# Sparse attention over 2708 rows on one core: the fullest tiles' last slots as a tile of their own, light tiles first, more turning on VectorE, s3 and C22 on GpSimd

## The chip, the cores and the metric

The kernel runs on one core of a Trainium2 chip. The metric is the device time of one execution in microseconds. A core has TensorE (PE, with its weight loads as PEld), VectorE (DVE), ScalarE (ACT), GpSimd (POOL) and SyncE (SP, which here only issues DMAs).

## The reference

```python
h = jnp.maximum(_layernorm(x, axis=-1), 0.0)      # x: 2708 x 1024
q = h @ W_q.T + b_q
k = h @ W_k.T + b_k
v = h @ W_v.T + b_v
z = scale * (q @ k.T)
spare_z = z * adj                                 # adj: 2708 x 2708 of 0 and 1, density 0.0014771
spare_z = jnp.where(spare_z == 0.0, -10000.0, spare_z)
attn = jax.nn.softmax(spare_z, axis=1)
out = x + jax.nn.relu(attn @ v)
```

A row has some four neighbours on average. So the scores are only worked out at the edges, and the sum over neighbours is taken over rows of h; the product with W_v comes after it.

## The kernel before, in words

The rows are sorted by their number of neighbours in two groups (tiles 0 to 7, and 8 to 21), 128 rows to a tile. `K[t]` is the number of neighbour slots of tile t: 15, 7, 6, 5, 4, 4, 3, 2 for the first group and 15, 7, 6, 6, 5, 5, 4, 4, 4, 3, 3, 2, 1, 0 for the second. Tiles 0 and 8 are the fullest.

**TensorE.** After a stage on the weights (until about 100 us), the work goes in 20 units of two row tiles each, then one tile alone. Ten q units multiply h by M = W_q'W_k (with what belongs to it); ten o units multiply u, the weighted sums of neighbour rows, by W_v. A unit is a 2 x 2 block product with seven instead of eight products (`multiply`, L1027 to L1050): operands a11, a12, a22 and the sums s1 to s4, weights M and T (T is `wlow` in the trace), banks X, Y, Z (`ps`, `psy`). Each product is an `add_block`, which the trace shows as 8 matmul records of L987. The results are C11, C12 (`c12`, L1071 for q and L1102 for o: Z plus u2), C22 (`c22`, L1068 and L1098: Y plus p5) and C21. In the o units, ACT copies Y first (`taken`), and VectorE adds p5.

**Turning.** The operands are needed transposed. A tile that is not *faced* is turned by PE (`pt<-ident,u`, eight matmuls, L405), ACT copies a11, a12 and a22 from PSUM (L705), and VectorE forms s1 and s3 from the transposed block in PSUM (L709). A tile in `FACED` is copied in another order by ACT (v, L921), stored in `u_dram`, read back by four DMAs of 128 KB (`by_quarters`, L682 to L687, tile `or`), and turned by VectorE in 32 x 32 squares (`STREAM_TRANSPOSE`, L692). Ten tiles are faced: 6, 5, 4, 3, 2, 0, 1, 20, 18, 19. In `lower` (L725 to L737) s1 = a22 + a21, s3 = a11 − a21, s2 = s1 − a11, s4 = a12 − s2. If a tile of the unit is faced, s2 and s4 run on GpSimd, and s3 on VectorE (L729); else all four run on VectorE.

**The attention stream.** For each tile: `fetch` asks for its q rows (pq) and neighbour rows, `fill` (L839) has GpSimd gather one slot of 128 rows of h at a time (L600, 512 KB) into 13 row buffers (g0 to g10 and two in M's place), `scores` (L854) makes one VectorE operation per slot (`junk`, L860, with an accumulator), ACT takes the exponent, `weights` (L880) normalises, `sums` (L909) adds one slot per VectorE operation (u, L913). A tile of more than 8 slots scores its first slots, gives their buffers back, and gathers those rows again for the sum. The generator `attention` does this in the order of the list `order` (6, 5, 4, 3, 2, 0, 1, 7, 13, 12, 11, 10, 14, 9, 15, 16, 20, 17, 18, 19, 8); it also sets the o units' pairs, and tile 8 is the one alone. `advance(share)` (L1210 to L1213 for the share) lets the stream go on by some 20 / 7 or 19 / 7 us in each of the seven steps of a unit, less 0.75 / 7 for each faced tile of the next unit. VectorE executes in that order, by hand.

**Around it.** GpSimd also adds x to each result by a gather with addition (`add_x`, L1086, y) and scatters it (L812, out_dram), all in program order. Stores of q rows (L1061), reads of pq (L833), the read-back of u (L687) and the loads of the W_v weights into M and T (L1292: M00, T0, T1, M10, M11, T2, T3 in steps of the last q unit) go through SyncE in program order.

Of the kernel before, what the change touches and what calls it, by code (L numbers as in the profile page):

```python
# [10 lines left out]
FT = mybir.dt.float32  # L11
# [26 lines left out]
FACED = (6, 5, 4, 3, 2, 0, 1, 20, 18, 19)  # L38
# [28 lines left out]
def tile_preln_masked_attention(  # L67
# [25 lines left out]
    K = slot_counts(EARLY * P, EARLY) + slot_counts(N - EARLY * P, FULL - EARLY)[:-1] + [1, 0]  # L93
    PW = N // PARTS
# [12 lines left out]
    u_dram = dram.tile([FULL * P, D], FT, name="u_dram")  # L107
    m_dram = dram.tile([2, 2, P, 4, NB], FT, name="m_dram")
# [515 lines left out]
    def reload(lo, hi):  # L624
# [4 lines left out]
        if hi > FULL:  # L629
            loads.append(nc.gpsimd.dma_start(ptab[:REST, FULL, :], src[(FULL - lo) * P:, :]))  # L630
# [67 lines left out]
    def blocks(xa, xb, eng=None):  # L698
# [25 lines left out]
        def lower():  # L724
            if is_faced(xb):  # L725
# [3 lines left out]
                behind.append(nc.vector.tensor_sub(ops["s3"], ops["a11"], ops["s3"]))  # L729
# [94 lines left out]
    def fetch(t):  # L824
# [54 lines left out]
    def weights(t):  # L879
# [7 lines left out]
        if t in EMPTY:  # L887
# [12 lines left out]
        else:  # L900
            with tc.issue_after(chain[-1].ins):
                nc.vector.scalar_tensor_tensor(w[:, :k], w[:, :k], 1.0, ok, op0=ALU.mult, op1=ALU.mult, accum_out=m[:, 1:2])
                nc.vector.reciprocal(m[:, 3:4], m[:, 1:2])
                chain.append(nc.vector.tensor_scalar(coef[:, :k], w[:, :k], m[:, 3:4], None, op0=ALU.mult))  # L904
            nc.scalar.activation(u, g_of[t][0], AF.Copy, scale=coef[:, at[t][0]:at[t][0] + 1])  # L905
            free.append(g_of[t][0])
        us[t] = u, coef

    def sums(t):  # L909
        u, coef = us.pop(t)  # L910
        for s in range(0 if t in EMPTY else 1, K[t]):
            fill()
            chained(lambda: nc.vector.scalar_tensor_tensor(  # L913
                u, g_of[t][s], coef[:, at[t][s]:at[t][s] + 1], u, op0=ALU.mult, op1=ALU.add))
# [611 lines left out]
```

## Time and profile before

| what | value |
|---|---|
| median of 3 runs | 644.42 us (643.57 to 645.74) |
| the profiled execution's own time | 642.46 us |
| its span | 640.7 us |
| mean granted TensorE clock | 0.996 |
| bytes moved by DMA | 189.00 MB |
| gathers of h into g and M | 105 and 20 |
| DMAs issued by SyncE to read u back, of 128 KB | 40 |

A line of the timeline has the start and the length in us, the engine, the line of kernel.py, the operation, out<-in, the shape, and in brackets the idle time of the engine ahead of it with what ended it. A group's line has the count, then busy us and the mean ns of one, then idle time with its releasers.

### The profile page before, as it was taken

The numbers are of one execution on the slowest core, as the hardware profiler recorded it, in microseconds if no ns is written. First come the engines' busy times: TensorE is split into PE (matmuls) and PEld (weight loads), VectorE is DVE, ScalarE is ACT, GpSimd is POOL, SyncE is SP. The second block draws the span as 40 slices with busy tenths as digits, with TensorE's granted clock in tenths as the row PEclk, the third lists the DMA queues.
The fourth block names the chain that finished last, engine by engine and source line by source line (L and its number), as shares of the span: only waits on it lengthen the run. The fifth ranks groups of instructions, "written<-read, shape, count | busy, mean of one in ns | idle before, by whom it ended". The sixth has DMA issues, their size and how long they took to land.

```text
span 640.7 us, 6299 instructions
## 1 busy us (share of the span) xinstructions
PE 630.0 (98%) x1651; PEld 318.6 (50%) x1651; DVE 535.9 (84%) x1022; ACT 282.2 (44%) x420; POOL 398.4 (62%) x412
## 2 busy tenths in 40 slices
PE   9999999999999999999999989999999999999996
PEld 5777766444445444444444434444444434444442
DVE  5999889897895765989888998899999989999621
ACT  3448984859675532434232123333342426422300
POOL 2649960975768457745744836578674877873533
PEclk9999999999999999999999989999999999999999
DMA  8999996598798969997996999998997999986354
GB/s 337 406 352 319 352 361 265 203 342 317 248 367 311 369 194 401 371 370 249 274 310 243 326 419 288 343 277 251 341 313 251 270 346 289 283 266 193 72 164 145
DMA packets 66305, 189.00 MB, mean 295 GB/s; under 512 B 11181, under 2 KB 16637, under 8 KB 65368
## 3 DMA queue, kind: packets, MB, share of 16 engines
q0 software_dynamic: 27888, 84.95, 41.8%
q1 hardware_dynamic: 32874, 84.12, 37.5%
q10 hardware_dynamic: 5502, 19.48, 7.7%
q8 instruction: 15, 0.25, 0.2%
q14 instruction: 26, 0.21, 0.1%
HBM read 159.81 MB, written 42.31 MB: 315 GB/s over the span
## 4 chain that ended last, share of the span: by engine, by line
PE 18%; DVE 16%; issue 12%; DMA 9%; POOL 4%; ACT 0%; POOLq 0%; DVEq 0%
PE ps L987 10%; PE psy L987 7%; DVE junk L860 6%; DVE u L913 6%; DMA g<-h_dram,tab 3%; DMA pq<-q_late 3%; POOL g L600 2%; DMA or<-u_dram 2%; DMA qr<-h_dram,tab 2%; DVE s L709 1%; POOL M L600 1%; DMA pq<-q_dram,tab 1%; PE pt L405 1%; POOL qr L602 0%; DVE a L692 0%
## 5 line engine op out<-in xcount | busy, mean ns | idle before, releaser
L600 POOL DMA_INDIRECT g<-h_dram,tab x105 | 128.0, 1219 | 53.4 <-issue 19.2
L987 PE MATMUL ps<-M,a 128*128 128x512 f32 x320 | 145.8, 599 | 2.8 <-DMA M<-in_wv_dram 2.8
L987 PE MATMUL psy<-wlow,s 128*128 128x512 f32 x320 | 143.9, 592 | 0.0
L860 DVE SCALAR_TENSOR_TENSOR junk<-g,pq 128x1024 uint8<-128x1024 f32 x93 | 115.9, 1246 | 3.5 <-DMA g<-h_dram,tab 1.0
L913 DVE SCALAR_TENSOR_TENSOR u<-g,coef,u 128x1024 f32<-128x1024 f32 x79 | 106.1, 1343 | 5.2 <-ACT u L905 3.1
L987 PEld LDWEIGHTS ps<-M,a 128*128 128x128 f32 x320 | 60.1, 192 | 73.9 <-issue 69.9
L987 PEld LDWEIGHTS psy<-wlow,s 128*128 128x128 f32 x320 | 59.6, 190 | 69.7 <-issue 68.9
L379 DVE FIND_INDEX8 at<-ones,adj 128x8 uint32<-128x685 f32 (+1 forms) x88 | 74.5, 864 | 0.0
L987 PE MATMUL ps<-wlow,s 128*128 128x512 f32 x160 | 72.0, 593 | 1.2 <-DVE s L709 1.2
L987 PE MATMUL psy<-wlow,a 128*128 128x512 f32 x160 | 72.0, 593 | 0.0
L987 PE MATMUL ps<-M,s 128*128 128x512 f32 x160 | 71.9, 592 | 0.0
L358 ACT ACTIVATE sized<-adj 128x2708 uint8<-128x2708 f32 (+1 forms) x22 | 54.2, 2466 | 6.7 <-DMA adj<-in_adj_dram 5.4
L288 POOL TENSOR_TENSOR hsum<-hsum,x 128x256 f32<-128x256 f32 (+1 forms) x56 | 38.6, 724 | 26.6 <-DVE wlow L434 22.1
L987 PEld LDWEIGHTS ps<-wlow,s 128*128 128x128 f32 x160 | 30.3, 190 | 39.7 <-issue 39.3
L987 PEld LDWEIGHTS psy<-wlow,a 128*128 128x128 f32 x160 | 30.3, 190 | 38.5 <-issue 36.8
L987 PEld LDWEIGHTS ps<-M,s 128*128 128x128 f32 x160 | 30.3, 190 | 38.3 <-issue 37.5
L1086 POOL DMA_INDIRECT y<-in_x_dram,tab x19 | 31.0, 1633 | 14.7 <-issue 4.4
L812 POOL DMA_INDIRECT out_dram<-y,tab x21 | 27.9, 1330 | 15.4 <-DMA y<-in_x_dram,tab 9.9
L600 POOL DMA_INDIRECT M<-h_dram,tab x20 | 22.9, 1145 | 12.8 <-ACT u L905 4.7
L616 POOL DMA_INDIRECT tab_dram<-tab,pos_i x22 | 22.4, 1018 | 11.7 <-DVE pos_i L676 6.2
L266 ACT ACTIVATE x<-x,r 128x1024 f32<-128x1024 f32 (+1 forms) x22 | 25.8, 1232 | 6.1 <-POOL r L256 6.1
L905 ACT ACTIVATE u<-g,coef 128x1024 f32<-128x1024 f32 x16 | 18.4, 1148 | 21.9 <-DVE coef L904 20.8
(240 smaller groups left out, 871.4 us busy)
## 6 DMA issues: line engine op xcount, KB each, us to landing
adj<-in_adj_dram SPq DMA_DIRECT2D x21, 1354.0 KB, 12.2
x<-in_x_dram SPq DMA_DIRECT2D x21, 512.0 KB, 11.0
h_dram<-x ACTq DMA_DIRECT2D x21, 512.0 KB, 7.4
q_late<-q SPq DMA_DIRECT2D x12, 512.0 KB, 4.6
pq<-q_late SPq DMA_DIRECT2D x12, 512.0 KB, 4.9
u_dram<-v ACTq DMA_DIRECT2D x10, 512.0 KB, 5.6
or<-u_dram SPq DMA_DIRECT2D x40, 128.0 KB, 12.2
g<-in_wv_dram SPq DMA_DIRECT2D x16, 256.0 KB, 8.3
```

What stands on the lines that cost most here:

```text
L266: nc.scalar.activation(xs[i][:n], xs[i][:n], AF.Relu, bias=r[:n, 4, i:i + 1], scale=r[:n, 3, i:i + 1])
L288: small.append(nc.gpsimd.tensor_add(hsum[:n, cols], hsum[:n, cols], xt[:n, cols]))
L358: nc.scalar.activation(sized[:n], a[:n, :, :PW], AF.Abs, accum_out=total[:n, t:t + 1])
L379: nc.vector.max_index(at[:n, k - first_k, g, :], ones[:n, 0:8], a[:n, g, :])
L600: return nc.gpsimd.indirect_dma_start(out=dst, out_offset=None, in_=src, in_offset=off, bounds_check=N - 1, oob_is_err=False)
L616: put = nc.gpsimd.indirect_dma_start(out=tab_dram[lo >= EARLY][:, :], out_offset=bass.IndirectOffsetOnAxis(ap=pos_i[:n, t:t + 1], axis=0), ...
L812: to = nc.gpsimd.indirect_dma_start(out=out, out_offset=bass.IndirectOffsetOnAxis(ap=ptab.bitcast(U32)[:n, t, SLOTS:SLOTS + 1], axis=0), i ...
L860: chained(lambda: nc.vector.scalar_tensor_tensor(junk, g_of[t][s], 1.0, tq[t], op0=ALU.mult, op1=ALU.mult, accum_out=zall[:, t, s:s + 1]))
L905: nc.scalar.activation(u, g_of[t][0], AF.Copy, scale=coef[:, at[t][0]:at[t][0] + 1])
L913: chained(lambda: nc.vector.scalar_tensor_tensor(u, g_of[t][s], coef[:, at[t][s]:at[t][s] + 1], u, op0=ALU.mult, op1=ALU.add))
L987: mm = nc.tensor.matmul(bank, a[:, c, :], b[:, c, :], start=False, stop=(c == 3), skip_group_check=True)
L1086: return nc.gpsimd.indirect_dma_start(out=y[:n], out_offset=None, in_=x, in_offset=off, compute_op=ALU.add)
```

## The change

Four things are done together.

- *A second tile.* `K[0]` and `K[8]` become 8. Slots 8 to 14 of the first 64 rows of tiles 0 and 8 form tile 21 (`SECOND`, 7 slots; upper half of the partitions from tile 8, `HP` = 64). It is treated by the attention stream just ahead of tile 0: its weighted sum is not normalised and goes to `v_dram`, its sum of weights (`mass`) is moved from partitions 64 to 127 to partitions 0 to 63 by a small DMA. Tiles 0 and 8 add the mass to theirs, and a last operation of 64 rows adds the rows read from `v_dram`. No tile gathers rows twice any more (14 gathers fewer, and 7 more for tile 21).
- *The order* becomes 6, 5, 4, 3, 2, 1, 0, 7, 20, 19, 18 and so on down to 9, and 8 alone.
- *Faced tiles* are found as the stream goes: every tile finished before step 2 of the unit two ahead of its own. This makes 18; tiles 11, 9 and 8 are not faced.
- *GpSimd* takes s3 of faced units (L743 now) and C22 of the o units (L1140 now). The share of an o unit's steps is 19 / 7 always. The q rows of tiles 18 and 19 are stored through ACT's queue.

The diff, cut to its core:

```diff
-FACED = (6, 5, 4, 3, 2, 0, 1, 20, 18, 19)
...
+    HOSTS = (0, EARLY)
+    SECOND = NT - 1
+    HP = P // 2
+    VK = K[0] - WIDE
+    for t in HOSTS:
+        K[t] = WIDE
...
+        loads.append((nc.gpsimd if lo >= EARLY else nc.sync).dma_start(
+            ptab[part, SECOND, 0:SLOTS + 1 - WIDE], src[0:HP, WIDE:SLOTS + 1]))
...
-                behind.append(nc.vector.tensor_sub(ops["s3"], ops["a11"], ops["s3"]))
+                nc.gpsimd.tensor_sub(ops["s3"], ops["a11"], ops["s3"])
...
+        if t == SECOND:
+            gather(tq[t][:HP], q_dram[:, :], t, SLOTS - WIDE, HP)
+            nc.sync.dma_start(tq[t][HP:], q_late[:HP, :])
...
+            if s == K[t]:
+                half = slice(HOSTS.index(t) * HP, (HOSTS.index(t) + 1) * HP)
+                nc.gpsimd.dma_start(g[:HP], v_dram[half, :])
...
-            if s < k - WIDE:
-                free.append(g_of[t][s])
...
-        if k > WIDE:
-            g_of[t] = g_of[t][k - WIDE:]
-            wanted.extend((t, s) for s in range(k - WIDE))
...
+        if t == SECOND:
+            coef = w
+            with tc.issue_after(chain[-1].ins):
+                chain.append(nc.vector.scalar_tensor_tensor(w[:, :k], w[:, :k], 1.0, ok, op0=ALU.mult, op1=ALU.mult,
+                                                            accum_out=mass[:, 0:1]))
+            nc.sync.dma_start(mass[:HP, 1:2], mass[HP:, 0:1])
...
+                if t in HOSTS:
+                    second = HOSTS.index(t)
+                    nc.vector.tensor_add(m[:HP, 1:2], m[:HP, 1:2], mass[:HP, second:second + 1])
...
+        if t in HOSTS:
+            chained(lambda: nc.vector.scalar_tensor_tensor(
+                u[:HP], g_of[t][K[t]][:HP], m[:HP, 3:4], u[:HP], op0=ALU.mult, op1=ALU.add))
...
+        if t == SECOND:
+            nc.sync.dma_start(v_dram, u)
+            return
+        unit = next((n for n, pair in enumerate(units) if pair[0] == "o" and t in pair[1:]), len(units))
+        if now < [unit - 2, 2] and t != alone:
+            faced_tiles.add(t)
+        if t in faced_tiles:
...
-    order = [6, 5, 4, 3, 2, 0, 1, 7, 13, 12, 11, 10, 14, 9, 15, 16, 20, 17, 18, 19, 8]
+    order = [6, 5, 4, 3, 2, 1, 0, 7, 20, 19, 18, 17, 16, 15, 14, 13, 12, 11, 10, 9, 8]
...
-    stream = attention(order)
+    stream = attention(order[:order.index(0)] + [SECOND] + order[order.index(0):])
...
-            (nc.scalar if t < 4 else nc.sync).dma_start(dst, q)
+            (nc.scalar if t < 4 or t >= BARE - 2 else nc.sync).dma_start(dst, q)
...
-            nc.vector.tensor_add(p5, copied(Y), p5)
+            nc.gpsimd.tensor_add(p5, copied(Y), p5)
...
-            share -= 0.75 / 7 * len(set(nxt[1:]) & set(FACED))
+            share = 19.0 / 7
```

Three places show how the order of instructions changes. The first is GpSimd's between the results of the first two o units (units 10 and 11), where the operands of unit 12 are formed. Here y is an add_x, out_0_dram a scatter, g and M gathers of neighbour rows. Before:

```order
L1086 DMA y_5_2445<-in_x_dram,tab_97 128x1024
L812 DMA out_0_dram<-y_6_2444,tab_97 2708x1024
L709 TENSOR_TENSOR s2_2622<-s1_2619,a11_2585 128x512
L709 TENSOR_TENSOR s4_2624<-a12_2587,s2_2622 128x512
L600 DMA g7_1406<-h_dram_63,tab_97 128x1024
L1086 DMA y_4_2577<-in_x_dram,tab_97 128x1024
L812 DMA out_0_dram<-y_5_2445,tab_97 2708x1024
L600 DMA M_145<-h_dram_63,tab_97 128x1024 x2
L600 DMA g8_1407<-h_dram_63,tab_97 128x1024
```

After the change:

```order
L611 DMA g1_1405<-h_dram_63,tab_98 128x1024
L611 DMA g3_1407<-h_dram_63,tab_98 128x1024
L743 TENSOR_TENSOR s3_2645<-a11_2593,s3_2645 128x512
L723 TENSOR_TENSOR s2_2650<-s1_2647,a11_2593 128x512
L723 TENSOR_TENSOR s4_2652<-a12_2595,s2_2650 128x512
L1140 TENSOR_TENSOR p5_2552<-taken_2710,p5_2552 128x512
L611 DMA g4_1408<-h_dram_63,tab_98 128x1024
L1128 DMA y_4_2563<-in_x_dram,tab_98 128x1024
L826 DMA out_0_dram<-y_5_2444,tab_98 2708x1024
L611 DMA g5_1409<-h_dram_63,tab_98 128x1024
L611 DMA g6_1410<-h_dram_63,tab_98 128x1024
L611 DMA g7_1411<-h_dram_63,tab_98 128x1024
```

s3 now stands ahead of s2 and s4, and the C22 of unit 11 (p5 with taken) behind them; the gathers g4 to g7 follow it in the queue, where before g7 and two gathers into M came right after s4.

The second place is VectorE's in a later o unit: the lower operands of unit 16 (before tiles 14 and 9, now 16 and 15) are formed while unit 15's C12 is due. Here pt is a transposed block in PSUM, `or` a tile read back, junk2 a score, u_ a sum, u2 of ps1 the C12. Before:

```order
L913 TENSOR_SCALAR u_16_3237<-M_145,coef_3236,u_16_3237 128x1024 x2
L913 TENSOR_SCALAR u_16_3237<-g8_1407,coef_3236,u_16_3237 128x1024
L709 TENSOR_TENSOR s1_3275<-a22_3268,pt_3270 128x512
L709 TENSOR_TENSOR s3_3277<-a11_3226,pt_3270 128x512
L709 TENSOR_TENSOR s2_3279<-s1_3275,a11_3226 128x512
L709 TENSOR_TENSOR s4_3281<-a12_3233,s2_3279 128x512
L860 TENSOR_SCALAR junk2_3288,zall_102<-g10_1409,pq_17_3242 128x1024
L860 TENSOR_SCALAR junk2_3290,zall_102<-g0_1399,pq_17_3242 128x1024
L1102 TENSOR_TENSOR u2_3259<-ps1_3135,u2_3259 128x512
```

After the change:

```order
L941 TENSOR_SCALAR u_12_3209<-g4_1408,coef_3208,u_12_3209 128x1024
L941 TENSOR_SCALAR u_12_3209<-g5_1409,coef_3208,u_12_3209 128x1024
L941 TENSOR_SCALAR u_12_3209<-g6_1410,coef_3208,u_12_3209 128x1024
L706 STREAM_TRANSPOSE a22_3256<-or_15_3167 128x4x4x32
L706 STREAM_TRANSPOSE s3_3258<-or_15_3167 128x4x4x32
L723 TENSOR_TENSOR s1_3260<-a22_3256,s3_3258 128x512
L941 TENSOR_SCALAR u_12_3209<-g7_1411,coef_3208,u_12_3209 128x1024
L881 TENSOR_SCALAR junk2_3279,zall_103<-g0_1404,pq_10_3228 128x1024
L1144 TENSOR_TENSOR u2_3246<-ps1_3143,u2_3246 128x512
```

Two transposes from `or_15` and one addition stand where four additions and subtractions stood; s3, s2 and s4 are no longer in VectorE's list.

The third place is SyncE's around the loads of the W_v weights (`wlow` is T, M from `in_wv_dram` the halves M10 and M11). Before:

```order
L687 DMA or_3_2379<-u_dram_66 32x4x256 x4
L1292 DMA wlow_168<-tv_dram_68 128x2048
L1061 DMA q_late_65<-q_18_2325 128x1024
L1292 DMA M_145<-in_wv_dram 128x2048 x2
L1292 DMA wlow_168<-tv_dram_68 128x2048
L1061 DMA q_late_65<-q_19_2326 128x1024
L1292 DMA wlow_168<-tv_dram_68 128x2048
```

After the change:

```order
L1103 DMA q_late_65<-q_17_2152 128x1024
L1335 DMA wlow_172<-tv_dram_69 128x2048
L1335 DMA M_149<-in_wv_dram 128x2048
L906 DMA mass_115<-mass_115 64x1
L701 DMA or_4_2378<-u_dram_66 32x4x256 x4
L701 DMA or_3_2383<-u_dram_66 32x4x256 x4
L954 DMA v_dram_67<-u_21_2355 128x1024
L1335 DMA M_149<-in_wv_dram 128x2048
L1335 DMA wlow_172<-tv_dram_69 128x2048 x2
```

T1 and M10 now follow the store of q_17 directly, without the store of q_18 ahead of M10; M11, T2 and T3 follow the move of mass, the read-back of tiles 4 and 3, and the store of u_21.

More of the change, by code (lines that the diff above doesn't have):

```diff
@@ L159, in tile_preln_masked_attention @@
     msq = const.tile([P, 9 + NT], FT, name="msq")
+    mass = const.tile([P, 2], FT, name="mass")
     nc.vector.tensor_copy(past, rows_i)
@@ L1203, in tile_preln_masked_attention @@
         kind, ta, tb = unit
-        now[0] = n
+        now[:] = n, 0
         if n == FIRST:
```

48 lines of the change are left out of this document (32 added, 16 removed).

## The prediction

> **What bounds the kernel now.** First the busy times of the page, then the windows of the o units (345 to 597 us) and of the tail.
>
> ```profile
> PE 630.0 (98%) x1651; PEld 318.6 (50%) x1651; DVE 535.9 (84%) x1022; ACT 282.2 (44%) x420; POOL 398.4 (62%) x412
> 345.00:597.00 252.00, 247.80 (x633) 113.39 (x632) 239.24 (x357) 83.52 (x143) 171.01 (x126) 0.99 0.93 294
> 597.00:640.70 43.70, 38.42 (x97) 17.11 (x95) 11.74 (x28) 6.55 (x12) 16.15 (x14) 0.98 0.50 140
> ```
>
> The columns of a window are its length and the busy time of PE, PEld, DVE, ACT and POOL, then the granted clock, the DMA share and GB/s. PE is busy 98% of the span, so the kernel looks bound by TensorE. But between 345 and 597 us VectorE is busy for 239.24 of 252 us: it has 13 us to spare in nine units. Whatever takes work from PE here must leave VectorE able to follow.
>
> PE's timeline gives the pace and the stalls.
>
> ```profile
> 427.73 1.04 PE L405 MATMUL pt<-ident,u 128*128 128x128 f32 x8
> 428.61 3.60 PE L987 MATMUL ps<-M,a 128*128 128x512 f32 x8
> 432.04 3.60 PE L987 MATMUL ps<-M,s 128*128 128x512 f32 x8
> ...
> 505.52 1.07 PE L405 MATMUL pt<-ident,u 128*128 128x128 f32 x8 [0.27 <-DVE u L913]
> ...
> 521.48 3.67 PE L987 MATMUL ps<-wlow,s 128*128 128x512 f32 x8 [1.15 <-DVE s L709]
> ...
> 377.86 5.40 PE L987 MATMUL ps<-M,a 128*128 128x512 f32 x8 [2.77 <-DMA M<-in_wv_dram]
> ```
>
> A product takes 432.04 − 428.61 = 3.43 us, so the seven of a unit take 24.0. Turning one tile on PE takes 428.61 − 427.73 = 0.88. There are three stalls in the o units: 0.27 for a u, 1.15 for an s1, and 2.77 for the half M10 of the Wv weights. The last also left the next product at 5.40 instead of 3.60 us, a lower granted clock, so it cost 4.6.
>
> The third thing to read is how far VectorE runs behind PE. C12 of a unit waits for the product in Z.
>
> ```profile
> 354.76 3.17 PE L987 MATMUL ps<-M,s 128*128 128x512 f32 x7
> 357.76 3.60 PE L987 MATMUL psy<-wlow,s 128*128 128x512 f32 x8
> 361.46 0.68 DVE L1071 TENSOR_TENSOR q<-ps,u 128x512 f32<-128x512 f32 x1
> ...
> 585.98 3.60 PE L987 MATMUL ps<-M,s 128*128 128x512 f32 x8
> 597.86 0.68 DVE L1102 TENSOR_TENSOR u<-ps,u 128x512 f32<-128x512 f32 x1
> ```
>
> In unit 9 Z was complete at about 357.9 and VectorE took it at 361.46, 3.6 late. In unit 18 it was complete at 589.6 and taken at 597.86, 8.3 late. VectorE took nine units in 597.86 − 361.46 = 236.4 us, 26.3 each. It already falls behind PE, and the s1 of the next unit, which stands just ahead of C12 on VectorE, is wanted by PE two products (6.9) after Z. With the C12 after it and an interleaved u, I put the largest lag PE can stand without stalls at some 11.5 us.
>
> **The change, part by part.** Durations, by form:
>
> ```profile
> L405 PE MATMUL pt<-ident,u 128*128 128x128 f32 x88 | 11.4, 273 | 0.3 <-DVE u L913 0.3
> L860 DVE SCALAR_TENSOR_TENSOR junk<-g,pq 128x1024 uint8<-128x1024 f32 x93 | 115.9, 1246 | 3.5 <-DMA g<-h_dram,tab 1.0 <-DMA pq<-q_dram,tab 0.7
> L913 DVE SCALAR_TENSOR_TENSOR u<-g,coef,u 128x1024 f32<-128x1024 f32 x79 | 106.1, 1343 | 5.2 <-ACT u L905 3.1 <-ACT u L899 0.2
> L1098 DVE TENSOR_TENSOR p<-taken,p 128x512 f32<-128x512 f32 x9 | 6.2, 688 | 1.2 <-ACT taken L1052 1.1
> L709 DVE TENSOR_TENSOR s<-a,pt 128x512 f32<-128x512 f32 x32 | 20.5, 681 | 6.2 <-ACT a L705 6.2
> L692 DVE STREAM_TRANSPOSE a<-or 128x512 f32<-128x512 f32 x16 | 10.6, 692 | 0.9 <-DMA or<-u_dram 0.9
> L709 POOL TENSOR_TENSOR s<-a,s 128x512 f32<-128x512 f32 x8 | 14.8, 1856 | 0.6
> L600 POOL DMA_INDIRECT g<-h_dram,tab x105 | 128.0, 1219 | 53.4 <-issue 19.2 <-ACT u L905 15.6 <-DVE u L913 11.8
> L1086 POOL DMA_INDIRECT y<-in_x_dram,tab x19 | 31.0, 1633 | 14.7 <-issue 4.4 <-DMA tail_dram<-y 4.1 <-ACT y L1103 3.2
> L812 POOL DMA_INDIRECT out_dram<-y,tab x21 | 27.9, 1330 | 15.4 <-DMA y<-in_x_dram,tab 9.9 <-issue 5.5
> ```
>
> *PE.* Eight more tiles are turned by VectorE: 64 matmuls fewer, 8 × 0.88 = 7.0 us, all on the path while PE sets the pace. The stalls of 0.27 and 1.15 may go with them. Together **−8.4**. The 4.6 for M10 is open on both sides.
>
> ```profile
> 362.20 0.34 SPq L1061 DMA_DIRECT2D q_late<-q  x1
> 362.63 2.60 SPq L1292 DMA_DIRECT2D M<-in_wv_dram  x2
> ```
>
> On SyncE's queue M10 and M11 were issued right behind the store of q_18, which waited for VectorE's operation at 361.46. M10 no longer stands behind it, but M11, T2 and T3 now stand behind the store of u_21, whose last sums come two steps after that same C12, near 366. I keep the 4.6, with 0 and 2 us more as ends.
>
> *VectorE, from C12 of unit 9 to C12 of unit 18.* By its order of instructions before and now, this stretch holds 73 and 67 scores, 65 and 58 sums (two of them of 64 rows): tile 8 takes 8 slots instead of 15, and tile 0's end and the last two sums of tile 21 fall here. A score costs 1.27 (1.246 and what its accumulator's read adds): −6 × 1.27 = −7.6; sums −7 × 1.34 = −9.4. Nine C22 go to GpSimd: −6.2. The newly turned tiles drop s<-a,pt 8 times, and 7 more subtractions go to GpSimd: −15 × 0.68 = −10.2. 16 transposes come: +16 × 0.69 = +11.0. Sum **−22.4**.
>
> Against this stands what GpSimd's work costs VectorE while both run. Before, GpSimd ran 12 subtractions in six pairs beside VectorE. The second and the last pair, with the operation of VectorE beside them, and the same operations undisturbed:
>
> ```profile
> 408.83 1.69 POOL L709 TENSOR_TENSOR s<-s,a 128x512 f32<-128x512 f32 x1 [3.58 <-DVE s L709]
> 410.60 2.13 POOL L709 TENSOR_TENSOR s<-a,s 128x512 f32<-128x512 f32 x1
> 592.96 1.69 POOL L709 TENSOR_TENSOR s<-s,a 128x512 f32<-128x512 f32 x1 [7.65 <-DVE s L709]
> 594.73 2.13 POOL L709 TENSOR_TENSOR s<-a,s 128x512 f32<-128x512 f32 x1
> 375.15 1.22 DVE L860 SCALAR_TENSOR_TENSOR junk<-g,pq 128x1024 uint8<-128x1024 f32 x1
> 409.32 2.29 DVE L860 SCALAR_TENSOR_TENSOR junk<-g,pq 128x1024 uint8<-128x1024 f32 x1
> 411.54 2.27 DVE L913 SCALAR_TENSOR_TENSOR u<-g,coef,u 128x1024 f32<-128x1024 f32 x1
> 593.44 4.49 DVE L913 SCALAR_TENSOR_TENSOR u<-g,coef,u 128x1024 f32<-128x1024 f32 x2
> 589.48 1.28 DVE L913 SCALAR_TENSOR_TENSOR u<-g,coef,u 128x1024 f32<-128x1024 f32 x1
> ```
>
> A junk takes 2.29 instead of 1.22 and a u 2.27 instead of 1.28: the pair at 409 costs VectorE 1.07 + 0.99 = 2.06, the one at 593 costs 4.49 − 2.56 = 1.93. Some pairs fell beside other work and cost less, so I take 0.88 an operation, between 0 (only transposes and operands in PSUM beside it) and 1.03 (the pair at 409). GpSimd gets 25 operations more (9 C22, 8 s3, and an s2 and an s4 in each of four units), of which 24 fall in the stretch: 24 × 0.88 = **+21.1**, ends 0 and +24.7. VectorE's net is −22.4 + 21.1 = **−1.3**: what was taken from it is handed back as waiting. Its stretch becomes 235.1, 26.1 a unit.
>
> This is the page "SBUF — State Buffer" of the Trainium skill, section "Who interferes with whom": VectorE and GpSimd share one port pair as an exclusive lock, and a VectorE instruction with two SBUF inputs contends with a GpSimd instruction that reads SBUF, one with at most one such input does not. The rows just shown agree (2.29 against 1.22 us), and it speaks against moving s3 and C22: by it only an operation that meets such an instruction has a price. If the 8 s3 met nothing but transposes, the sum would be 16 × 0.88 = 14.1 instead of 21.1.
>
> *GpSimd.* From the add_x of tile 6 to that of the 15th tile, seven units:
>
> ```profile
> 389.88 1.62 POOL L1086 DMA_INDIRECT y<-in_x_dram,tab  x1 [1.92 <-issue]
> ...
> 575.89 1.58 POOL L1086 DMA_INDIRECT y<-in_x_dram,tab  x1 [0.30 <-issue]
> ...
> 395.22 1.01 POOL L600 DMA_INDIRECT g<-h_dram,tab  x1 [0.30 <-issue]
> ```
>
> Before they took 186.0 us and held, by the order of GpSimd's instructions, 66 gathers, 14 add_x, 13 scatters and 6 subtractions. With 0.30 of issue ahead of each DMA and 0.08 between the two subtractions at 409, that is 66 × 1.52 + 14 × 1.93 + 13 × 1.63 + 6 × 1.94 = 160.2, 26 us below the time. After they hold 54, 15, 14 and 26: 54 × 1.52 + 15 × 1.93 + 14 × 1.63 + 26 × 1.94 = **184.3**. With the cheapest of each that the rows show (a gather of 1.31 with its issue, a subtraction of 1.77) it is 54 × 1.31 + 29.0 + 22.8 + 26 × 1.77 = 168.6. PE's seven units are 7 × 24.0 = 168. So at the mean prices GpSimd needs 16 us more than PE gives it, and can borrow them only from a lead of at most 13 row buffers (13 × 1.52 = 20 us).
>
> *Rest.* 18 instead of 10 ACT copies v (1.05 us) lie on an engine busy 83.52 of 252 us: nothing. 32 more 128 KB reads by SyncE replace 8 whole ones; same bytes. 21 fewer gathers of 512 KB relieve a DMA share of 0.93. The gather of tile 21's pq and the move of mass lie in the q units beside PE's work: nothing, about 2 us if VectorE waits for them.
>
> **Sum.** PE would save 8.4, but VectorE follows at 26.1 us a unit and GpSimd at 184.3 / 7 = 26.3. VectorE ends 1.3 earlier, and if its lag may grow from 8.3 towards 11.5, PE ends up to 4.5 earlier; GpSimd at 184.3 against 186.0 ends 1.7 earlier, and at its cheap end it binds nothing. I take **−3.0**, the middle of −1.3 and −4.5. The profiled execution took 642.46 (span 640.7 and 1.8 around it): 639.5. The median of the three runs, 644.42, lies 2.0 above: 644.42 − 3.0 = **641.4**. This case runs from −7 to +1: a price of 0.70 or 1.03 for 0.88 moves VectorE's 24 operations by −4.3 or +3.6.
>
> **The rivals.**
> - *PE stays the bound*, if the operations meet transposes and PSUM operands so that VectorE gives back under 8 us: −8.4, or −13.0 with M10 in time, so 636.0 to 631.4, middle 633.7. For it: GpSimd's cheap end. Against it: all the heavy pairs shown met a junk or a u, which fill 222 of VectorE's 536 us.
> - *GpSimd's queue becomes the pace: slower.* It works in order. C22 waits there for ACT's copy of Y, s3 and s2 for s1 by VectorE, and behind them stand the gathers that VectorE's scores wait for, which in turn hold up s1. Before, one wait for s1 was 3.58, another 7.65 us, in slack. With 184.3 of work the point is reached when more than 1.7 of such waiting in seven units finds no slack. At 1 us in each of nine units, less 1.7 × 9 / 7 = 2.2, it is +6.8; I take +6: 650.4. Against it: the lead of 13 buffers.
> - *The weights come late* behind u_21 (2 us more, and about as much given back of the forecast): about 644.4, no change.
>
> **How the numbers follow.** Forecast 0.48; PE the bound 0.15; GpSimd's queue 0.31; weights 0.06. About 0.3% (1.9 us) is what a measurement of this kernel can tell from no change. Of the forecast's −7 to +1, 0.31 lies below −1.9, 0.15 within, 0.02 above. Faster 0.31 + 0.15 = 0.46; same 0.15 + 0.06 = 0.21; slower 0.02 + 0.31 = 0.33. The range reaches from 633 (most of PE's case) to 651 (most of the queue's). The likeliest case alone: 637.4 to 645.4.
>
> **What would show it.** Right: PE's pt<-ident,u down to 24, with stalls of 0.5 to 1.5 us in several o units released by VectorE's s or GpSimd's s; junk and u above 2 us beside nearly every GpSimd operation; C12 of unit 18 some 10 us after Z; POOL above 90% busy with its issue gaps. Wrong: PE without stalls and the end 8 us earlier; or C12 later each unit with VectorE waiting for gathers, and GpSimd idle on ACT's copy.

## The result and the profile after

The changed kernel takes 675.55 us (674.41 to 679.98, 4 runs) against 644.35 us (4 runs): a ratio of 1.050, with a 95% interval of 1.046 to 1.054. It is 31 us slower, where 3 us less were forecast. The profiled execution took 674.51 us, its span is 672.8 us, the mean granted clock 0.970.

First the busy times of the changed kernel's page, then the window from the T3 product of unit 12 to that of unit 17, with the columns of before.

```profile
PE 633.4 (94%) x1587; PEld 315.6 (47%) x1587; DVE 533.1 (79%) x999; ACT 284.8 (42%) x418; POOL 421.8 (63%) x420
448.70:603.40 154.70, 131.28 (x290) 57.22 (x289) 128.39 (x177) 45.52 (x74) 119.01 (x84) 0.91 0.94 279
```

The columns of the second line are those of the prediction's windows: the length, the busy time of PE, PEld, DVE, ACT and POOL, the granted clock, the DMA share and GB/s. PE works 131.28 of 154.70 us, at a mean clock of 0.91. VectorE is idle for 26 of these 155 us and GpSimd for 36. No engine is full in this stage: they wait for each other. PE's timeline, cut to its stalls from unit 9 on, says where.

```profile
370.21 3.70 PE L1029 MATMUL psy<-wlow,a 128*128 128x512 f32 x8 [1.83 <-DVE q L1110]
...
383.86 6.65 PE L1029 MATMUL ps<-M,s 128*128 128x512 f32 x8 [3.08 <-DMA M<-in_wv_dram]
...
454.92 5.25 PE L1029 MATMUL psy<-wlow,s 128*128 128x512 f32 x8 [2.62 <-issue]
460.01 3.60 PE L1029 MATMUL ps<-M,a 128*128 128x512 f32 x8
...
487.88 5.84 PE L1029 MATMUL psy<-wlow,s 128*128 128x512 f32 x8 [7.10 <-issue]
493.56 3.60 PE L1029 MATMUL ps<-M,a 128*128 128x512 f32 x8
...
551.17 6.62 PE L1029 MATMUL ps<-M,s 128*128 128x512 f32 x8 [5.95 <-ACT p L1045]
557.62 3.60 PE L1029 MATMUL psy<-wlow,s 128*128 128x512 f32 x8
...
579.26 6.22 PE L1029 MATMUL psy<-wlow,s 128*128 128x512 f32 x8 [7.74 <-issue]
585.33 1.04 PE L416 MATMUL pt<-ident,u 128*128 128x128 f32 x8
```

Four stalls stand in the o units: 2.62 + 7.10 + 5.95 + 7.74 = 23.4 us idle. The product behind each is slow as well: it takes 5.09, 5.68, 6.45 and 6.07 us from its start to the next one's, where 3.43 is the pace, 9.6 us more; the granted clock in these four stretches was 0.69, 0.62, 0.54 and 0.58. Together 33.0 us.

ScalarE's timeline around the second, third and fourth of these:

```profile
485.11 0.63 ACT L1141 ACTIVATE y<-p 128x512 f32<-128x512 f32 x1 [12.31 <-POOL p L1140]
...
487.21 0.57 ACT L1042 COPY psy<-ps 128x512 f32<-128x512 f32 x1
487.72 0.58 ACT L1045 COPY p<-ps 128x512 f32<-128x512 f32 x1
...
549.92 0.63 ACT L1141 ACTIVATE y<-p 128x512 f32<-128x512 f32 x1 [6.42 <-POOL p L1140]
550.46 0.56 ACT L1045 COPY p<-ps 128x512 f32<-128x512 f32 x1
...
578.05 0.63 ACT L1141 ACTIVATE y<-p 128x512 f32<-128x512 f32 x1 [13.05 <-POOL p L1140]
578.58 0.58 ACT L1042 COPY psy<-ps 128x512 f32<-128x512 f32 x1
```

ScalarE stands for 12.31 us at its relu of C22, which waits for GpSimd's addition. Behind it in the queue are the copies of X to Y (`psy<-ps`) and of Z to p5 (`p<-ps`) for the next unit. PE's s2 T1 goes into that Y: it starts at 487.88, 0.1 behind the end of that copy (487.21 + 0.57), and at 579.26, 0.1 behind 578.58 + 0.58. s4 M11 goes into Z and starts at 551.17, 0.15 behind 550.46 + 0.56. The answer to who waits for GpSimd's C22 gives the sums:

```profile
L1140 POOL TENSOR_TENSOR p<-taken,p x9: 1274/1484/2252, 395.5 to 622.8; 128x512 f32<-128x512 f32 x9
...
  ACT y L1141: 48.9, 9
...
  PE psy L1029: 17.5, 3
```

All nine relus waited, 48.9 us in all, and PE's three stalls that the profile calls "issue" (17.5 us) are traced through ScalarE to this line; the fourth, of 5.95 us, follows ScalarE's copy of Z in the rows above. GpSimd itself stood idle for only 0.2 us in all ahead of the nine additions. Why was it late? Its timeline ahead of the second stall:

```profile
458.60 1.56 POOL L1128 DMA_INDIRECT y<-in_x_dram,tab  x1 [0.30 <-ACT v L962]
467.30 0.98 POOL L826 DMA_INDIRECT out_dram<-y,tab  x1 [7.14 <-DMA y<-in_x_dram,tab]
468.59 1.51 POOL L611 DMA_INDIRECT g<-h_dram,tab  x1 [0.30 <-issue]
...
476.62 0.99 POOL L611 DMA_INDIRECT g<-h_dram,tab  x1 [0.30 <-issue]
477.64 1.27 POOL L743 TENSOR_TENSOR s<-a,s 128x512 f32<-128x512 f32 x1
478.86 1.27 POOL L723 TENSOR_TENSOR s<-s,a 128x512 f32<-128x512 f32 x1
480.21 2.13 POOL L723 TENSOR_TENSOR s<-a,s 128x512 f32<-128x512 f32 x1
482.50 1.01 POOL L611 DMA_INDIRECT g<-h_dram,tab  x1 [0.15 <-DVE w L924]
483.54 1.54 POOL L1140 TENSOR_TENSOR p<-taken,p 128x512 f32<-128x512 f32 x1
```

A scatter waited 7.14 us for its add_x to land; behind it came six gathers, s3, s2, s4, one more gather, and only then C22, at 483.54. Ahead of the fourth stall there is no such wait: C22 comes at 576.74, behind 13 us of s3, s2, a gather, s4, an add_x, a scatter and a gather that follow each other from 563.82 on. There it is the place of C22 in the queue alone.

The 32.1 us between the two spans add up: unit 9 ends 2.2 later (370.21 against 368.06, VectorE's C22 of q); the late weights, now M11 instead of M10, cost 1.5 more (6.1 against 4.6); the four stalls 33.0; less 7.0 for turning and 1.4 for the old stalls. That makes 28.3, and PE's last unit does end its T3 product 649.75 − 621.30 = 28.45 later. The rest, 3.65, lies behind the last scatter:

```profile
664.88 0.96 POOL L1369 DMA_INDIRECT out_dram<-y_alone,half_i  x1 [1.67 <-DVE y_alone L1385]
```

From its start to the end of the span it is 7.9 us, where it was 4.3 before (636.43 to 640.7).

### The profile page after: what moved, and what is told of

It reads as the page before. It is cut to its first block, busy times and chain, and to the rows that moved or that the text cites. A ratio compares the mean times of both kernels' runs of the same rounds, so it can differ in the third digit from the quotient of the medians.

```text
span 672.8 us, 6187 instructions
## 1 busy us (share of the span) xinstructions
PE 633.4 (94%) x1587; PEld 315.6 (47%) x1587; DVE 533.1 (79%) x999; ACT 284.8 (42%) x418; POOL 421.8 (63%) x420
## 2 busy tenths in 40 slices
DMA packets 69697, 191.64 MB, mean 285 GB/s; under 512 B 10855, under 2 KB 20407, under 8 KB 68760
## 4 chain that ended last, share of the span: by engine, by line
PE 16%; DVE 14%; issue 13%; DMA 9%; POOL 7%; ACT 2%; POOLq 0%; SPq 0%; DVEq 0%; ACTq 0%
PE ps L1029 9%; PE psy L1029 6%; DVE junk L881 5%; DVE u L941 5%; DMA g<-h_dram,tab 3%; POOL g L611 2%; DMA M<-in_wv_dram 2%; DVE a L706 1%; POOL y L1128 1%; DMA qr<-h_dram,tab 1%; DMA M<-h_dram,tab 1%; POOL s L723 1%; DMA or<-u_dram 1%; POOL M L611 1%; DMA pq<-q_dram,tab 1%
## 5 line engine op out<-in xcount | busy, mean ns | idle before, releaser
L1029 PE MATMUL psy<-wlow,s 128*128 128x512 f32 x320 | 150.4, 615 | 17.5 <-issue 17.5
L1029 PE MATMUL ps<-M,a 128*128 128x512 f32 x320 | 144.1, 593 | 0.0
L611 POOL DMA_INDIRECT g<-h_dram,tab x87 | 108.8, 1250 | 42.1 <-issue 15.9
L881 DVE SCALAR_TENSOR_TENSOR junk<-g,pq 128x1024 uint8<-128x1024 f32 x86 | 111.4, 1295 | 14.7 <-DMA g<-h_dram,tab 12.3
L1029 PEld LDWEIGHTS psy<-wlow,s 128*128 128x128 f32 x320 | 62.1, 198 | 94.3 <-issue 93.9
L941 DVE SCALAR_TENSOR_TENSOR u<-g,coef,u 128x1024 f32<-128x1024 f32 x64 | 92.0, 1438 | 8.5 <-ACT u L930 4.4
L1029 PE MATMUL ps<-M,s 128*128 128x512 f32 x160 | 78.0, 634 | 9.0 <-ACT p L1045 6.0
L1029 PEld LDWEIGHTS ps<-M,s 128*128 128x128 f32 x160 | 32.4, 204 | 51.0 <-issue 50.8
L826 POOL DMA_INDIRECT out_dram<-y,tab x21 | 27.6, 1313 | 35.0 <-DMA y<-in_x_dram,tab 18.6
L1128 POOL DMA_INDIRECT y<-in_x_dram,tab x19 | 34.0, 1790 | 20.6 <-ACT y L1153 11.9
L962 ACT COPY v<-u 128x1024 f32<-128x1024 f32 x18 | 18.8, 1045 | 23.8 <-DVE u L941 23.8
```

The lines of the kernel that those rows point to most:

```text
L611: return nc.gpsimd.indirect_dma_start(out=dst, out_offset=None, in_=src, in_offset=off, bounds_check=N - 1, oob_is_err=False)
L826: to = nc.gpsimd.indirect_dma_start(out=out, out_offset=bass.IndirectOffsetOnAxis(ap=ptab.bitcast(U32)[:n, t, SLOTS:SLOTS + 1], axis=0), i ...
L881: chained(lambda: nc.vector.scalar_tensor_tensor(junk, g_of[t][s], 1.0, tq[t], op0=ALU.mult, op1=ALU.mult, accum_out=zall[:, t, s:s + 1]))
L941: chained(lambda: nc.vector.scalar_tensor_tensor(u, g_of[t][s], coef[:, s:s + 1], u, op0=ALU.mult, op1=ALU.add))
L962: nc.scalar.copy(v.rearrange("p (a c r) -> p c a r", a=QUADS, r=QP), u.rearrange("p (c a r) -> p c a r", a=QUADS, r=QP))
L1029: mm = nc.tensor.matmul(bank, a[:, c, :], b[:, c, :], start=False, stop=(c == 3), skip_group_check=True)
```

## The experiments

All ratios are to the kernel before, run on the same chip as the experiment, with 95% intervals. Six theories were on trial: **A**, ScalarE's queue (its relu of C22 waits for GpSimd and holds up copies that PE needs); **B**, the amount of GpSimd's work; **C**, VectorE's waiting at the port that it shares with GpSimd; **D**, the order of the tiles; **E**, the second tile or the late M11; **F**, the stream's rate.

**e1 to e4: GpSimd's two jobs, and ScalarE's order alone.** e1 puts C22 back on VectorE, e2 s3, e3 both:

```diff
-            nc.gpsimd.tensor_add(p5, copied(Y), p5)
+            nc.vector.tensor_add(p5, copied(Y), p5)
...
-                nc.gpsimd.tensor_sub(ops["s3"], ops["a11"], ops["s3"])
+                behind.append(nc.vector.tensor_sub(ops["s3"], ops["a11"], ops["s3"]))
```

e4 leaves both on GpSimd and moves only the relu in ScalarE's list, from `c22` to `c21` and behind the copy of Z to p5 of the next unit (`copies[-1]`):

```diff
-            nc.scalar.activation(yb[:, hi], p5, AF.Relu)
+            late.append(p5)
...
             nc.scalar.activation(yb[:, lo], Y, AF.Relu)
+            with tc.issue_after(copies[-1].ins):
+                nc.scalar.activation(yb[:, hi], late.pop(), AF.Relu)
```

> The kernel after the change, with C22 of the o units added by VectorE again instead of GpSimd; all else stays. Theory A (ScalarE's queue): four of the new stalls of TensorE in the o units (2.62, 7.10, 5.95 and 7.74 us, and some 9.5 us of lower clock behind them, 33 us in all) come because ScalarE's relu of C22 waits for GpSimd's addition, and the copies of X to Y and of Z to p5 for the next unit stand behind that relu on ScalarE. Then they go: 675.5 - 33 = about 643 (639 to 648). Theory B (GpSimd simply has too much to do, whatever it is): taking 9 of its 37 operations gives back about a quarter: 665 to 670. Theory C (VectorE loses its time to GpSimd at their shared port): 9 x 0.88 = 8 us less of waiting, 9 x 0.69 = 6 us more of work: 673 to 677.

> The kernel after the change, with s3 of the faced units formed by VectorE again; C22 stays on GpSimd. Theory A: the relu still waits for GpSimd, but one operation of about 2 us less stands ahead of C22 in GpSimd's queue in each unit: 4 stalls shorter by 2 to 4 us each with their clock, 660 to 670. Theory B: 8 to 10 operations fewer, like the run with C22 on VectorE: 665 to 670. Theory C: 672 to 677.

> The kernel after the change, with both C22 and s3 on VectorE as before the change. What is left is the second tile, the light tiles first and 18 faced tiles. Theory A: like the run with C22 alone on VectorE, or a little below: 637 to 645, since 7 us of TensorE's turning are saved and VectorE has 16 us less of scores and sums. Theory B: 640 to 650. A fourth theory D (the order of tiles or the late M11 and not GpSimd causes the loss) gives 660 or more.

> The kernel after the change, with C22 and s3 on GpSimd as they are; only ScalarE's relu of C22 is issued behind the copies X to Y and Z to p5 of the next unit instead of ahead of them. GpSimd's and VectorE's lists stay the same. Theory A: TensorE no longer waits for these copies: 643 to 652. Theory B and theory C, in which it is GpSimd's or VectorE's work that is late: no change, 670 to 680.

Measured: e1 658.39 us, ratio 1.0208 (1.0151 to 1.0265); e2 670.65, 1.0419 (1.0367 to 1.0471); e3 657.14, 1.0226 (1.0182 to 1.0269); e4 665.35, 1.0333 (1.0291 to 1.0374). C22 alone is worth some 19 us (1.050 to 1.021 of 644), s3 alone some 5 (its interval just touches that of the changed kernel), both no more than C22. Theory C does not name the loss: e1 gave VectorE back its additions and was 2.9% faster. e4 changes nothing but ScalarE's order and gives 1.7% (11 us), which B and C do not. So A holds as one cause, but not for the size that it gave: moving the relu brings a third to a half of what A expected, and e1 and e3 end 10 and 12 us above A's ranges. In e4 PE's waits show what came next:

```profile
PE psy L1029 <- ACT u L1074: 9.9, 4, 4.4
PE ps L1029 <- DVE a L706: 5.9, 1, 5.9
```

The copy of u2 now holds PE, 9.9 us in four stalls. In two of them (4.44 and 0.93 us) ScalarE had stood at the relu, which is later now; in the other two (3.89 and 0.69 us) it had waited for VectorE's scores and sums. The 5.9 us are VectorE's transpose.

And e1 and e3 are 15 and 14 us above before without any C22 on GpSimd. A part of that can be seen. In e1:

```profile
441.35 1.23 DVE L881 SCALAR_TENSOR_TENSOR junk<-g,pq 128x1024 uint8<-128x1024 f32 x1 [9.98 <-DMA pq<-q_late]
443.35 2.05 PE L1029 MATMUL ps<-M,a 128*128 128x512 f32 x2 [8.94 <-DVE a L706]
```

VectorE waits 9.98 us for the q rows of its next tile. The transposes of a tile read back stand behind that score in its list, and PE waits 8.94 us for them. In e3 the same two waits are 4.82 and 4.12 us. Before, VectorE never waits for rows of `q_late`; e18 (the new order alone, below) does so for 4.8 us. How much of the 14 us this makes is not shown.

**e5 to e8: the order of the tiles, and each of GpSimd's jobs in the kernel before.** e5 is e3 with the order of before (tile 21 ahead of tile 0), e6 the changed kernel with that order; e7 and e8 are the kernel before with one edit each.

> The kernel after the change with C22 and s3 on VectorE, and the tiles in the order of before (tile 21 ahead of tile 0); 13 tiles come out as faced instead of 18. Theory D (the light tiles first cost the 14 us that were left with C22 and s3 on VectorE: their q rows come too late, and the heavy tiles at the end overload VectorE): the second tile saves VectorE 16 us and TensorE turns three tiles fewer than before, 638 to 645. Theory E (the second tile or the late M11 costs them): 650 to 658, as in the new order.

> The kernel after the change with C22 and s3 on GpSimd as changed, but the tiles in the order of before. Theory A (ScalarE's queue behind GpSimd's C22) is independent of the order: 14 to 20 us above the same order with both on VectorE, 653 to 664. Theory D alone would give the time of that run, 638 to 645.

> The kernel before, with one edit: C22 of the o units is added by GpSimd. Theory A: ScalarE's relu waits for GpSimd in its queue and holds the copies for the next unit: 652 to 664. Theory B (the amount of GpSimd's work): GpSimd had 26 us to spare in seven units and gets 9 x 1.94 = 17 more, 642 to 647.

> The kernel before, with one edit: s3 of its five units with a faced second tile is formed by GpSimd. Every theory: s3 is wanted a whole unit later, so only s2 behind it is 2 us later and VectorE gives back what it saves: 642 to 647, no change.

Measured: e5 655.95 us, 1.0160 (1.0124 to 1.0196); e6 658.26, 1.0204 (1.0172 to 1.0236); e7 651.25, 1.0108 (1.0066 to 1.0150); e8 645.25, 1.0012 (0.9989 to 1.0036). e8 is as expected. e5 lies in theory E's range. e7, 1.1% slower, lies between B's range and A's. e6 refutes a part of A: in the order of before the same two jobs on GpSimd cost 0.4%, with intervals that overlap, not 14 to 20 us. That e6 lies in A's range of times is luck: it does so because e5 came out slow. Who waits for C22 in e6:

```profile
L1140 POOL TENSOR_TENSOR p<-taken,p x9: 1264/1401/2250, 398.5 to 607.7; 128x512 f32<-128x512 f32 x9
...
  ACT y L1141: 39.5, 8
  DVE s L706: 1.4, 1
```

ScalarE waits almost as long (39.5 against 48.9 us), but PE does not appear among those who wait. In e7 it is the same: seven relus wait 31.6 us, and no stall of PE is traced to them. Whether that wait reaches PE depends on what stands behind the relu and how late GpSimd is at that place. Nor does e5 take the remaining 14 us away: in the order of before it is still 12 us above before. Theory D alone falls. (e5 and e6 have 13 faced tiles, not 18, so the order is not all that differs.)

**e9 to e12: the rate of the stream.** The o units' share, and that of the last q unit, becomes 17 / 7:

```diff
-        share = (20.0 if kind == "q" else 19.0) / 7
+        share = (20.0 if kind == "q" else 17.0) / 7
...
-            share = 19.0 / 7
+            share = 17.0 / 7
```

e9 is e3 with it, e10 e5, e11 the changed kernel. e12 is the kernel before without its deduction for faced tiles. A slower stream also ends fewer tiles in time to be faced: by the stores to `u_dram` 16 in e9 and e11 instead of 18, and 11 in e10 instead of 13. So these three change two things.

> The kernel after the change with C22 and s3 on VectorE, new order of tiles, and the attention stream let on by 17 / 7 us a step in the o units (and the last q unit) instead of 19 / 7. Theory F (19 / 7 without the deduction for faced tiles asks more of VectorE than TensorE's 24 us a unit: 19 of stream, 2.8 of four transposes, 2.8 of s1, s3, C12 and C22, and 1.8 at the port are 26.4): two us a unit less, 6 to 12 us of the 14 are gained: 645 to 651. Without theory F (the stream is set by when the tiles are needed, or by the late q rows): 655 to 660.

> As the run with C22 and s3 on VectorE in the order of before, with 17 / 7 instead of 19 / 7. Theory F: 642 to 650. Otherwise 653 to 658.

> The kernel after the change as it is (C22 and s3 on GpSimd), with 17 / 7 instead of 19 / 7. Theory F alone: 10 us less, 663 to 668. Theory A (the chain over ScalarE's queue does not hang on VectorE's pace): 670 to 678.

> The kernel before, with one edit: the stream goes on by 19 / 7 us a step ahead of units with faced tiles too (no deduction of 0.75 / 7 for each). Theory F: up to 1.5 us a unit more asked in seven units, 3 to 8 us: 647 to 652. Otherwise 642 to 646.

Measured: e9 650.91 us, 1.0116 (1.0081 to 1.0151); e10 651.87, 1.0119 (1.0079 to 1.0159); e11 663.06, 1.0271 (1.0225 to 1.0318); e12 646.31, 1.0044 (1.0022 to 1.0067). Less stream per unit is faster with both on VectorE in the new order (1.1%) and in the changed kernel (2.3%); in the order of before the intervals overlap. e12 shows the same with the sign turned, 0.4%, just below the expected range. In e11 PE's stalls traced to C22 fall from 17.5 to 9.1 us, so A's chain does hang on the pace. What goes with the pace in the new order is how long GpSimd stands at its scatters until an add_x has landed. In the changed kernel:

```profile
L826 POOL DMA_INDIRECT out_dram<-y,tab x21 | 27.6, 1313 | 35.0 <-DMA y<-in_x_dram,tab 18.6 <-DVE flag L1360 8.7 <-issue 4.0
```

These 18.6 us were 9.9 before; they are 19.5 to 27.7 in e1 to e4, and 4.6 and 4.4 in e9 and e11. Why these landings are late is not shown: the DMA share was 1.05 over units 12 and 13 of e9 too, where PE lost nothing. The starts of the T3 product of some units tell where e9 wins and loses:

| unit | 9 | 11 | 13 | 15 | 16 | 17 | 18 | 19 |
|---|---|---|---|---|---|---|---|---|
| before | 368.06 | 420.87 | 471.56 | 524.99 | 550.77 | 575.68 | 599.72 | 621.30 |
| after | 370.21 | 424.67 | 477.18 | 534.76 | 567.92 | 603.37 | 628.28 | 649.75 |
| e3 | 371.31 | 420.87 | 476.02 | 526.00 | 555.21 | 584.57 | 609.58 | 631.06 |
| e9 | 369.78 | 421.90 | 470.85 | 518.91 | 543.82 | 568.97 | 599.12 | 623.74 |

At unit 17 e9 is 6.7 us ahead of before, and since unit 9 it has gained 8.4: seven tiles fewer turned by PE up to there (7 × 0.88 = 6.2), the old stalls (1.4), and 3.8 us for M11 where M10 cost 4.6. The lead is gone two units later. PE's stalls there:

```profile
578.60 1.06 PE L416 MATMUL pt<-ident,u 128*128 128x128 f32 x8 [2.50 <-DVE u L941]
...
595.58 3.70 PE L1029 MATMUL ps<-wlow,s 128*128 128x512 f32 x8 [2.19 <-DVE s L723]
...
606.53 1.06 PE L416 MATMUL pt<-ident,u 128*128 128x128 f32 x8 [2.96 <-DVE u L947]
```

PE waits for the sums of the heaviest tiles, 9 and 8, which this order puts last.

**e13 to e16: do the parts add up?** e13 is the edits of e4 and e11 together. e14 is the second tile alone in the kernel before (its stores of q 18 and 19 stay on ScalarE's queue). e15 is e9 at 18 / 7, e16 the same with tiles 18 and 17 moved to the end of the order. The faced tiles come out as 16, 10, 17 and 14.

> The kernel after the change (C22 and s3 on GpSimd) with both small edits together: ScalarE's relu of C22 behind the copies for the next unit, and the stream at 17 / 7. If theories A and F name the whole of what C22 and s3 on GpSimd cost, this comes to the run with both on VectorE at 17 / 7 (650.9): 648 to 655. If GpSimd's work has a further price of its own (the port, its own lateness), 657 to 663.

> The kernel before with the second tile alone: the order of before, the ten faced tiles of before, the deductions of before, C22 and s3 on VectorE (the stores of q 18 and 19 stay on ScalarE's queue). If the second tile itself costs little and the rest of the loss is the stream's rate and the newly faced tiles: 642 to 649, with VectorE done with tile 8 well before it is wanted. If the second tile is what costs (its work in the last q units, the Wv weights behind its store): 652 to 657.

> C22 and s3 on VectorE, new order, 18 / 7. With 17 / 7 TensorE was ahead of the kernel before until unit 17 and then waited for the heaviest tiles 9 and 8; with 19 / 7 VectorE fell behind earlier. If the two losses trade, the time lies at or a little below both: 648 to 654.

> As that, but with two light tiles at the end: order ... 20, 19, 16, 15, 14, 13, 12, 11, 10, 9, 8, 18, with 17 alone. If the wait for the heaviest tiles at the end costs the last 5 us: 641 to 647. If their weight only moves to the units before: 648 to 654.

Measured: e13 661.52 us, 1.0216 (1.0145 to 1.0287); e14 656.62, 1.0142 (1.0073 to 1.0211); e15 664.03, 1.0267 (1.0194 to 1.0339); e16 659.77, 1.0204 (1.0134 to 1.0274). On this chip the kernel before varied more (643.80 to 651.95), and the intervals are wide. e13 fell in its second range: the two edits together bring 2.8% of the 5.0%, not 3.8%, so GpSimd's jobs may have a further price, though its interval just overlaps that of e9. In e13 no stall of PE is traced to C22. e15 missed and limits theory F: 19 / 7 gives 1.0226, 18 / 7 1.0267, 17 / 7 1.0116. That isn't a curve of a rate. In e15 one wait of VectorE for a gathered row, 7.93 us, was followed by a stall of 8.07 us:

```profile
542.75 1.23 DVE L881 SCALAR_TENSOR_TENSOR junk<-g,pq 128x1024 uint8<-128x1024 f32 x1 [7.93 <-DMA g<-h_dram,tab]
548.36 6.38 PE L1029 MATMUL psy<-wlow,s 128*128 128x512 f32 x8 [8.07 <-ACT u L1073]
```

In between, ScalarE stood 11.16 us at the exponent of that tile's scores (547.62), and the copy of u2 that PE needs came right behind. This is the queue of theory A with another operation at its head, and no C22 on GpSimd. e16 missed: light tiles at the end did not help.

e14 fell in its second range, and is the run that matters here. Two windows of it, and about the same two stages of before, in the columns of before:

```profile
445.00:590.00 145.00, 138.42 (x367) 64.16 (x366) 136.79 (x226) 54.42 (x96) 84.85 (x66) 0.98 0.85 263
590.00:636.00 46.00, 46.00 (x115) 20.78 (x114) 8.52 (x15) 9.78 (x17) 17.63 (x15) 1.00 0.53 139
```

```profile
445.00:575.00 130.00, 128.57 (x354) 60.57 (x353) 123.64 (x209) 50.37 (x87) 93.03 (x70) 1.00 0.93 299
575.00:621.00 46.00, 46.00 (x114) 20.64 (x114) 30.42 (x42) 10.55 (x19) 19.64 (x15) 1.00 0.54 139
```

In the last 46 us VectorE's work falls from 30.42 to 8.52 us: that is what the second tile saves, and PE is busy for all of the 46 us in both. It is saved where nobody waits. In the stage before it VectorE is as full as ever (136.79 of 145). By the starts of T3 the profiled execution of e14 is 3.2 us behind before at unit 11 (424.02), 12.2 at unit 15 (537.22) and 12.1 at unit 19 (633.42). The rest of its 16.0 us lies behind the last scatter: 8.2 us to the end, where before had 4.3.

**e17 and e18: one part of the change each, in the kernel before.** e17 stores q 18 and 19 through ScalarE's queue; e18 takes the new order alone.

> The kernel before with one edit: the q rows of tiles 18 and 19 are stored through ScalarE's queue, so that M10 and M11 on SyncE's queue do not stand behind the store of q 18. If that store is why M10 came late (2.77 us of stall and 1.8 of lower clock), the 4.6 us go: 639 to 642, below both kernels. If M10 lands late because the DMA engines are full there (share 1.03), nothing changes: 643 to 646.

> The kernel before with one edit: the light tiles first (6, 5, 4, 3, 2, 1, 0, 7, 20, 19 down to 9, and 8 with its 15 slots alone); no second tile, the ten faced tiles of before, C22 and s3 on VectorE. If the order itself costs (q rows late at the light tiles, the heaviest last): 655 to 670, since tile 8's 29 operations now stand right before the end as before, but 9 and 10 too. If not: 643 to 648.

Measured: e17 646.21 us, 1.0007 (0.9981 to 1.0033), no change; e18 652.83, 1.0097 (1.0067 to 1.0127), a little under its expected range. In its profiled execution T3 of unit 17 starts at 576.21, only 0.5 us behind before; the loss comes at the very end, where PE waits for the last sum of tile 8, here with all its 15 slots:

```profile
622.09 1.94 PE L405 MATMUL pt<-ident,u 128*128 128x128 f32 x8 [5.33 <-DVE u L913]
```

So e18 does not price the order in the changed kernel, whose tile 8 has 8 slots. It also sends six tiles that are not faced through `u_dram` (195.30 MB moved, 6.3 more than before). In e17 the wait for M10 became several smaller ones:

```profile
376.27 3.67 PE L987 MATMUL psy<-wlow,s 128*128 128x512 f32 x8 [1.75 <-ACT ps L747]
380.84 3.70 PE L987 MATMUL ps<-M,a 128*128 128x512 f32 x8 [0.89 <-DMA M<-in_wv_dram]
385.40 3.67 PE L987 MATMUL ps<-M,s 128*128 128x512 f32 x8 [0.86 <-DMA M<-in_wv_dram]
389.33 3.67 PE L987 MATMUL psy<-wlow,s 128*128 128x512 f32 x8 [0.26 <-DMA wlow<-tv_dram]
```

No version was found that beats the kernel before.

## Why the prediction was wrong, point by point

- **The step that failed** is the cost of moving C22: "Nine C22 go to GpSimd: −6.2" on VectorE and 1.94 us each on GpSimd's account, and "18 instead of 10 ACT copies v lie on an engine busy 83.52 of 252 us: nothing". The result of C22 was not followed to its reader. Its reader is ScalarE, in order, with PE's next copies behind it. ScalarE is idle two thirds of the time and still stopped PE: the four stalls cost 33.0 us, 17.5 us of their idle time are traced to this line by name, and e4 wins 11 us with ScalarE's order alone. With C22 and s3 back on VectorE (e3) 18 of the 31 us are gone. In the order of before, where no stall of PE is traced to that wait, the same jobs cost only 0.4% (e6 against e5), and C22 alone 1.1% (e7).
- **GpSimd's queue as a rival** was the right direction, and had 0.31. Its price, +6, came from small waits at the pace of 1 us a unit and a lead of 13 buffers in gathers. A lead in gathers does nothing for C22, which cannot be done ahead. What was found was a scatter behind its add_x (7.14 us) with all that had piled up behind it, and 13 us of work ahead of C22. The sign that was named, GpSimd idle on ACT's copy, did not come; ScalarE waited for GpSimd instead.
- **Terms put at nothing.** The order of the tiles had no term, and the second tile only a gain. Apart from C22 and s3 these two and the faced tiles cost 14 us (e3), and e14, the second tile alone, is 1.4% slower. Nor does "32 more 128 KB reads by SyncE replace 8 whole ones; same bytes" hold: before, nothing was read back whole (10 stores to `u_dram`, 40 reads of 128 KB). Each newly faced tile adds a store and a read-back of 512 KB, and the bytes moved rose from 189.00 to 191.64 MB although there are 21 gathers fewer (125 and 104). What these bytes cost is not shown by itself.
- **PE's side** is borne out: −0.88 for each tile not turned fits e9, which gained 8.4 us on before from unit 9 to unit 17 with seven such tiles. The old stalls went as forecast, but larger ones came.
- **The clock** was left out of the price of a stall although the row of before showed it (2.77 idle cost 4.6): four stalls of 23.4 us cost 33.0.
- **VectorE's account** was a sum over nine units, and that hid a second mistake. Six scores and seven sums fewer lie mostly in tile 8 at the very end, where e14 shows them saved without use. (By the trace of before its stretch holds 66 sums, not 65, and eight of the nine C22; this moves the account by less than 1 us.) A total doesn't show in which unit an engine has the room.
- **The port's price** was too high. Two of the group rows of the changed kernel, to be held against those of before, then the same two of e3:

```profile
L881 DVE SCALAR_TENSOR_TENSOR junk<-g,pq 128x1024 uint8<-128x1024 f32 x86 | 111.4, 1295 | 14.7 <-DMA g<-h_dram,tab 12.3 <-DMA pq<-q_dram,tab 0.8
L941 DVE SCALAR_TENSOR_TENSOR u<-g,coef,u 128x1024 f32<-128x1024 f32 x64 | 92.0, 1438 | 8.5 <-ACT u L930 4.4 <-ACT u L921 2.7
...
L881 DVE SCALAR_TENSOR_TENSOR junk<-g,pq 128x1024 uint8<-128x1024 f32 x86 | 108.1, 1257 | 8.8 <-DMA pq<-q_late 4.8
L941 DVE SCALAR_TENSOR_TENSOR u<-g,coef,u 128x1024 f32<-128x1024 f32 x64 | 93.3, 1458 | 5.0 <-ACT u L930 2.4
```

  Mean times grew from 1.246 to 1.295 us for 86 scores, from 1.343 to 1.438 for 64 sums, and by 0.11 and 0.06 for the 31 with M, some 13 us in all, where 21.1 was forecast. With C22 and s3 back on VectorE (e3) a sum still takes 1.458, and of the 13 us some 8 stay; so only about 5 can be laid to these two. Whether that waiting reached PE no run tells; it is too small to be the loss.
- **The late weights** came as the ends allowed: M11 stalled 3.08 us and cost 6.1 in place of M10's 4.6. e17 shows that the store ahead of M10 was not what held it up by itself.

What stays open: why e14 loses 3 us in the q units and 9 in units 12 to 15; how much of e3's 2.3% is the second tile and how much the order and the newly faced tiles; why the add_x and single gathers land late, as in e15; and the last 3.6 us. The time from the last scatter to the end was 4.2 to 4.5 us in all six kernels without the second tile (before, e7, e8, e12, e17, e18), and 7.7 to 8.2 in all fourteen with it, e14 among them, with a DMA share of 0.01 in the last 4 us of the changed kernel. So these 3.6 us come with the second tile's program; no run tells through what.

## What to carry to other kernels

When a step moves to another engine, follow its result to the reader, and list what is queued behind that reader: an engine that is busy a third of the time can stop the one that sets the pace. Work that must come at a given moment does not belong behind a queue whose waits are long, even where its sum of work fits. And what is saved on a nearly full engine counts only in the units in which that engine is waited for; add up by unit, not over the stage.

## What the runs showed of the hardware that was not expected

After some stalls PE's next product ran slow, and not by the length of the stall: 2.62 us idle cost 1.7 more, 7.10 cost 2.3, 5.95 cost 3.0 and 7.74 cost 2.6, at granted clocks of 0.69, 0.62, 0.54 and 0.58, while stalls of 0.57 and 1.83 us left products of 3.70. Nor is there one length from which it happens: in e9 a stall of 2.02 us was followed by a product of 5.20 us at a clock of 0.67, in e18 stalls of 2.40 and 2.88 us by products of 3.51 and 3.53. The page "TensorE: Matmul & The Clock Gate" of the Trainium skill, section "What's actually happening", has the clock halve after an idle window of about 3.4 us; here 2.02 us of idle time was once enough.
